# Layer 1, end of the first feed-forward: eight passes over one sequence's rows, on VectorE instead of GpSimd

## The chip, the cores and the metric

The kernel runs on one core of a Trainium2 chip. The metric is the device time of one execution in microseconds (us). TensorE (PE in the profile) multiplies, VectorE (DVE), ScalarE (ACT) and GpSimd (POOL) work element by element, and SyncE (SP) starts transfers. Each engine takes its own instructions strictly in order; between engines they wait for one another through semaphores.

## The reference, cut to what matters

The reference is a model of four "macaron" layers, all in float32, on 4 sequences of 512 positions with 128 features (2048 rows). In each layer a feed-forward block is applied at half weight, then an attention, then the same feed-forward block again. Layer 1 is

```python
x = x + 0.5 * ffn(layernorm(x))     # the first feed-forward
x = x + attn(layernorm(x))          # linear attention
x = x + 0.5 * ffn(layernorm(x))     # the same again

def ffn(x):                          # L1_ffn
    x1  = layer_norm(x + masked_softmax_attention(x), ln1_w, ln1_b)
    g   = softmax(x1 @ gate_w.T + gate_b)               # 8 experts, the best 2 are kept
    moe = sum over the best 2 of g_e * (x1 @ expert_w[e] + expert_b[e])
    return layer_norm(x1 + moe, ln2_w, ln2_b)

def attn(x):                         # L1_attn, 16 heads of 8
    q, k, v = l2norm(x @ Wq), l2norm(x @ Wk), x @ Wv
    scores  = (q @ k.T) * sigmoid(x @ Wb + bb) * lower_triangle
    return (scores @ v) @ Wo
```

So each sequence passes through two normalizations with a weight and a bias (`ln1`, `ln2`) and one residual sum in each feed-forward block. These are the steps that the change touches.

## The kernel before, in words

The whole model is one program. `x` (the residual stream) and `y` (a work copy of the same shape) lie in on-chip memory as 128 partitions by 16 tiles by 128 features; one sequence `b` (0 to 3) is four of those tiles (`TB` = 4), that is 128 x 512 elements. `yb` and `xb` are the slices of one sequence.

The first feed-forward of layer 1 (`l1_ffn`, called "l1f") runs the masked attention sequence by sequence, heads in groups. When a sequence is done, `finish` adds the attention's result to `y` and calls `l1_experts(b)`. That function doesn't do its work at once. It puts a list of small steps on a *chain* of this sequence (`spare(gap, step)`), and the main loop's `tick()` runs the next step of each chain when its gap has passed. In this way the experts of one sequence are spread through the attention of the next ones. The last two sequences, 2 and 3, don't end in time for that: their chains are handed on to the next stage, the linear attention `l1_attn`, and go on between its steps. In that stage everything that VectorE and ScalarE are given stays in the order in which the program issues it (`ordered["dve"]`, `ordered["act"]`), and TensorE's products as well. GpSimd's instructions are placed by their dependences.

Names and lines of the profile that are needed below:

- `affine(n)`: `scaled_by_act` lets ScalarE subtract the mean and divide by the deviation, four tiles in place (L316), and then two passes over 128 x 512 elements multiply by the weight (L1149) and add the bias (L1150) on `eng`. `eng` is GpSimd for sequences 0 to 2.
- `residual()`: `x += y` for the sequence, L1229, on `eng`.
- For sequence 3 in the linear attention `normed_in_parts(n, gap)` does the same in smaller steps: statistics in two halves, the scaling on ScalarE in two pairs of tiles (L1246), then the weight (L1253) and the bias (L1254) on GpSimd. It is called for `ln1` and for `ln2`. The residual sum of sequence 3 is L1270.
- `leave_normed(b, ...)`: after the residual sum the statistics of `x` (the plain layer norm ahead of the next block), on VectorE, the root of the variance (L234 on POOL or on DVE, and the power on POOL, L235), the scaling to `y` on VectorE, and `turn(b)`, TensorE's transposes into `pt_y` with ScalarE's copy (L326).
- In `l1_attn`: `project` (`pq_1a` on PE, `sq` and `km` on ACT, L1326 and L1327), `roots` and `unit_norm` on DVE (`rn`, `ir`, `km`), `to_features` (`pt_1a` on PE, `qkT` and `qm` on ACT, L1380 and L1383), `scores` (`ps_1a` on PE; half of `PT` by DVE, half by ACT, L1400, and then a mask on POOL, L1401), `with_values` (`po_1a`, `pst` on PE; `state` on DVE and on POOL, L1428) and `output` (`pz_1a` on PE, the sum into `x` on DVE).

All of VectorE's instructions are recorded under L186 and TensorE's under L202 (products) and L199 (transposes), because helpers issue them.

Of the kernel before, what the change touches and what calls it, by code (L numbers as in the profile page):

```python
# [29 lines left out]
B, S, D, H, HD = 4, 512, 128, 16, 8  # L30
NT = B * S // P
TB = S // P
# [25 lines left out]
class Columns:  # L58
# [50 lines left out]
VEC = Columns([  # L109
    ("1f_bv", 128), ("1f_bo", 128), ("ln1w", 128), ("ln1b", 128), ("ln2w", 128), ("ln2b", 128),  # L110
    ("gate_b", 8), ("1a_bb", 16), ("2f_rb", 8), ("3a_bv", 128), ("3a_bo", 128),
    ("3f_s0", 256), ("3f_s1", 256),
])
# [4 lines left out]
def tile_macaron(ctx, tc, x_in, const_in, vec_in, w0_in, ws_in, ws3_in, w2f_in, w3_in, out):  # L118
    nc = tc.nc
# [38 lines left out]
    vec = keep.tile([P, VEC.n], F32, name="vec")  # L158
# [34 lines left out]
    vector = InOrder()  # L193
# [27 lines left out]
    def rows(ap, n):  # L221

        return ap[:, None, :].to_broadcast([ap.shape[0], n, ap.shape[1]])
# [58 lines left out]
    ordered, routed = {"act": False, "dve": False, "results": False}, {}  # L282

    def by_order(i):
        if ordered["act"]:
            tc.keep_in_program_order(i)

    def statistics_in_parts(src, b):

        got = []  # L290

        def half(i):
            if not i:
                for tag, shape, bufs in (("ln_st", [P, TB, 6], 2), ("ln_mv", [P, TB, 2], 3), ("ln_r", [P, TB], 3)):
                    got.append(keep.tile(shape, F32, tag=tag, name=tag, bufs=bufs))
            st, mv, r = got
            for t in (2 * i, 2 * i + 1):
                vector.bn_stats(st[:, t, :], src[:, b * TB + t, :])
                vector.bn_aggr(mv[:, t, :], st[:, t, :])
            if i:  # L300
                inverse_root(keep, r, mv[:, :, 1], "ir4", ALU.add, 1e-5, nc.gpsimd)

        return got, (lambda: half(0), lambda: half(1))

    def scaled_by_act(dst, src, b, stats):

        mv, r = stats
        m = keep.tile([P, TB], F32, tag="ln_m", name="ln_m", bufs=3)
        if gathering(b):
            vector.scalar_tensor_tensor(m, mv[:, :, 0], -1.0, r, ALU.mult, ALU.mult)  # L310
        else:
            nc.gpsimd.tensor_mul(m, mv[:, :, 0], r)
            nc.gpsimd.tensor_scalar_mul(m, m, -1.0)
        for i in range(TB):
            t = b * TB + i
            by_order(nc.scalar.activation(dst[:, t, :], src[:, t, :], AF.Identity, scale=r[:, i : i + 1], bias=m[:, i : i + 1]))  # L316
# [4 lines left out]
    def turn(b):  # L321

        pt = bank("m", "pt_y")
        for t in range(TB):
            transpose_in_order(pt[:, ts(t, P)], y[:, b * TB + t, :])
        by_order(nc.scalar.copy(yT[:, b, :], pt))  # L326
# [6 lines left out]
    def chain(b):  # L333
        parts = deque()
        chains.append([b, clock[0], parts])
        return lambda gap, f, products=True: parts.append((gap, f, products))
# [14 lines left out]
    def leave_normed(b, spare, gap, pinned=False, start=1, to_route=True):  # L351

        st = []

        def scale():
            scaled(y, x, b, st[-1] if pinned != "parts" else st[0][1:], pinned is True)
            ready.add(b)

        if pinned == "parts":
            got, halves = statistics_in_parts(x, b)  # L360
            st.append(got)
            spare(start, halves[0], False)
            spare(1, halves[1], False)
            spare(2, scale, False)
        else:
            spare(start, lambda: st.append(statistics(x, b)), False)
            spare(1, scale, False)
        spare(gap, lambda: turn(b))
        if routed and to_route:
            spare(1, lambda: logits(b))  # L370
            if b % 2:
                first, second, third = route(b // 2)
                spare(1, first, False)
                spare(routed["gaps"][0], second)
                spare(routed["gaps"][1], third)
# [715 lines left out]
    def l1_ffn(tag, xb, l1_tiles, begun=None, besides=()):  # L1091

        with pool(tag) as sb, banks(tag + "ps", **MIX):
# [35 lines left out]
            def finish(b, pr):  # L1129
                yb = y[:, ts(b, TB), :]  # L1130
                vector.tensor_add(yb, yb, pr)
                l1_experts(xb, b)
# [3 lines left out]
    def l1_experts(sb, b):  # L1136


        yb, xb = y[:, ts(b, TB), :], x[:, ts(b, TB), :]
        ew, eb = WS(ws, "ew"), WS(ws, "eb")  # L1140
        st = {}
        eng = vector if b == B - 1 else nc.gpsimd

        def statistics_of_y():
            st["y"] = statistics(y, b, eng)

        def affine(n):
            scaled_by_act(y, y, b, st["y"])
            eng.tensor_mul(yb, yb, rows(VEC(vec, f"ln{n}w"), TB))  # L1149
            eng.tensor_add(yb, yb, rows(VEC(vec, f"ln{n}b"), TB))  # L1150

        def gates():
            pl = bank("m", "pl")
# [43 lines left out]
        def products(t):  # L1197
            pe = two_banks("pe1")
            for half in range(2):
                mm_in_order(pe[half], yT[:, b, ts(t, P)], ew[:, ts(half, 512)])  # L1200
            st["pe", t] = pe

        def sum_up(pe, t, n, a=0):
            yt = y[:, b * TB + t, :]
            for e in range(a, n):
                vector.scalar_tensor_tensor(yt, pe[e // 4][:, ts(e % 4, D)], st["g"][:, t, e : e + 1], yt, ALU.mult, ALU.add)
# [19 lines left out]
            experts(t)  # L1226

        def residual():
            eng.tensor_add(xb, xb, yb)  # L1229

        def normed_in_parts(n, gap):

            got, halves = statistics_in_parts(y, b)
            m = []

            def means():
                _, mv, r = got
                m.append(keep.tile([P, TB], F32, tag="ln_m", name="ln_m", bufs=3))
                nc.gpsimd.tensor_mul(m[0], mv[:, :, 0], r)
                nc.gpsimd.tensor_scalar_mul(m[0], m[0], -1.0)  # L1240

            def scale(i):
                r = got[2]
                for t in (2 * i, 2 * i + 1):
                    yt = y[:, b * TB + t, :]
                    by_order(nc.scalar.activation(yt, yt, AF.Identity, scale=r[:, t : t + 1], bias=m[0][:, t : t + 1]))  # L1246

            spare(gap, halves[0], False)
            spare(1, halves[1], False)
            spare(1, means, False)  # L1250
            spare(1, lambda: scale(0), False)
            spare(1, lambda: scale(1), False)
            spare(0, lambda: nc.gpsimd.tensor_mul(yb, yb, rows(VEC(vec, f"ln{n}w"), TB)), False)  # L1253
            spare(1, lambda: nc.gpsimd.tensor_add(yb, yb, rows(VEC(vec, f"ln{n}b"), TB)), False)  # L1254

        spare = chain(b)
        if b == B - 1 and not routed:
            normed_in_parts(1, 1)
            spare(3, lambda: turn(b))
            spare(2, gates)  # L1260
            for f, gap in ((share, 1), (best, 1), (two_best, 1)):
                spare(gap, f, False)
            spare(1, turn_gates)
            spare(2, biases)
            for t in range(TB):
                spare(1, lambda t=t: products(t))
                spare(0, lambda t=t: sum_up(st["pe", t], t, 4), False)
                spare(1, lambda t=t: sum_up(st.pop(("pe", t)), t, 8, 4), False)
            normed_in_parts(2, 1)
            spare(1, lambda: nc.gpsimd.tensor_add(xb, xb, yb), False)  # L1270
            leave_normed(b, spare, 2, "parts", 2)
            return
        spare(2, statistics_of_y, False)
        spare(4, lambda: affine(1), False)
        spare(4, lambda: turn(b))
        alone = b == B - 1 and routed
# [10 lines left out]
        for t in range(TB):  # L1287
# [4 lines left out]
            else:  # L1292
                spare(2, lambda t=t: both(t))
        spare(1, statistics_of_y, False)
        spare(4, lambda: affine(2), False)
        spare(2, residual, False)
        leave_normed(b, spare, 2)

# [964 lines left out]
    with pool("ws") as wp:  # L2263
# [9 lines left out]
        with pool("l2x") as l2x:  # L2273
# [20 lines left out]
            with ExitStack() as first_layer:  # L2294
                xb = first_layer.enter_context(pool("l1x"))
# [43 lines left out]
            with pool("l2g") as sb, banks("l2gps", a=2, g=2, t=2, m=2):  # L2339
# [8 lines left out]
                while slots:  # L2348
                    n = slots[0][0]
# [163 lines left out]
```

## Time and profile before

| | |
|---|---|
| time, median of 4 runs | 2607.97 us (2600.35 to 2610.62) |
| the profiled execution: its time | 2608.76 us |
| the profiled execution: its span | 2606.9 us, so 1.9 us lie around the span |
| the linear attention of layer 1 in it | about 687.8 to 819.8 us of the span |
| in 680 to 820 us: busy PE, DVE, ACT, POOL | 103.6, 91.3, 66.4, 48.5 of 140 us |
| the eight passes that the change speaks of | 1.26 to 1.28 us each on POOL: five from 693.98 to 700.50 us, three from 755.97 to 759.91 us |

The profile's start times are us from the span's start. "busy" is the time in which an engine executes instructions, a "releaser" is the instruction that ended a wait, and PEclk is the clock that TensorE was granted, 1.00 being full speed. The share of an engine over the span says little here, since the change concerns some 70 us of 2607.

### The profile page before, as it was taken

Reading aid. Unit: us, or ns where it says so; the run is one execution under the profiler, and the core shown is the slowest. Engines: PE = TensorE matmul, PEld = TensorE weight load, DVE = VectorE, ACT = ScalarE, POOL = GpSimd, SP = SyncE. Lnnn points to the kernel's source line nnn. Section 1 sums busy time; section 2 is a strip of 40 time slices with the busy share of each in tenths; the row PEclk is TensorE's granted clock in tenths of the full one; section 3 lists DMA queues with packets and bytes.
Section 4 is the critical chain, followed back from the end, with each engine's and each line's share of the span. In section 5 each row is a group of like instructions: output and inputs, shape, how many; then the busy total and the mean of one; then the engine's idle time right before and its main releaser. Section 6 shows DMA issues by size and latency. Waiting matters only on the chain.

```text
span 2606.9 us, 50965 instructions
## 1 busy us (share of the span) xinstructions
PE 2235.9 (86%) x19070; PEld 1274.1 (49%) x19070; DVE 1776.9 (68%) x4755; ACT 1335.4 (51%) x3271; POOL 945.9 (36%) x1519
## 2 busy tenths in 40 slices
PE   5578679988778999988768868999889999799998
PEld 2245334443344444468648836555533333456555
DVE  3755667777466777755655478887557775888874
ACT  4056205444443544434526338887615555588874
POOL 2022113233232222333332368676310000777761
PEclk9789789899689999889969879999889999899998
DMA  3052000000000000037325821110000000110100
GB/s 150 0 170 92 1 0 2 1 1 2 1 1 1 2 2 5 23 122 239 100 87 157 273 67 26 24 26 20 3 1 1 1 1 1 29 28 22 24 22 13
DMA packets 40142, 113.21 MB, mean 43 GB/s; under 512 B 7064, under 2 KB 16536, under 8 KB 39384
## 3 DMA queue, kind: packets, MB, share of 16 engines
q1 hardware_dynamic: 36520, 100.94, 12.2%
q0 software_dynamic: 2944, 6.04, 1.1%
q8 instruction: 151, 2.47, 0.4%
q10 hardware_dynamic: 432, 2.98, 0.3%
q14 instruction: 95, 0.78, 0.1%
HBM read 79.78 MB, written 15.47 MB: 37 GB/s over the span
## 4 chain that ended last, share of the span: by engine, by line
PE 59%; DVE 19%; POOL 11%; ACT 6%; issue 4%; DMA 1%; SPq 0%; POOLq 0%; DVEq 0%; ACTq 0%
PE pk_at L202 11%; PE po_at L202 6%; PE pa L202 4%; PE pq_at L202 4%; PE pag L202 3%; DVE t L186 3%; PE pz L202 3%; PE po L202 3%; PE pe L202 3%; PE idle L202 2%; PE pg L202 2%; DVE y L186 2%; POOL t L1985 2%; PE p_qk L202 2%; PE pt L199 2%
## 5 line engine op out<-in xcount | busy, mean ns | idle before, releaser
L942 ACT ACTIVATE PT<-pk_at 128x512 f32<-128x512 f32 (+3 forms) x768 | 335.2, 488 | 377.9 <-PE pq_at L202 239.0
L202 PE MATMUL pk_at<-qx,km 32*128 32x512 f32 (+3 forms) x1536 | 400.3, 558 | 5.6 <-ACT PT L942 3.0
L186 DVE CUSTOM_DVE_ANT_0 s<-pq_at,cst 128x384 f32<-128x384 f32 (+3 forms) x512 | 249.9, 488 | 98.7 <-PE pq_at L202 45.3
L202 PE MATMUL pq_at<-km,qT 32*128 32x128 f32 (+3 forms) x1024 | 274.6, 504 | 15.6 <-DVE nm L186 12.5
L1927 ACT ACTIVATE s<-s,nm,rn 128x128 f32<-128x128 f32 x512 | 245.6, 483 | 5.5 <-DVE nm L186 5.3
L945 POOL TENSOR_SCALAR_AFFINE_SELECT PT<-PT 128x256 f32<-128x256 f32 x256 | 104.6, 411 | 384.1 <-ACT PT L942 382.8
L202 PEld LDWEIGHTS pk_at<-qx,km 32*128 32x128 f32 x1536 | 146.8, 191 | 155.0 <-issue 90.8
L202 PE MATMUL po_at<-PT,vh 128*32 128x128 f32 (+3 forms) x2432 | 203.2, 393 | 3.4 <-POOL PT L945 3.3
L186 DVE TENSOR_REDUCE nm<-pq_at 128x1 f32<-128x512 f32 x256 | 164.9, 685 | 52.2 <-PE pq_at L202 50.8
L186 DVE TENSOR_TENSOR t<-p_qk,w 128x512 f32<-128x512 f32 (+1 forms) x192 | 155.2, 862 | 52.4 <-ACT sq L1927 50.1
L1985 POOL TENSOR_TENSOR t<-t,t 128x1024 f32<-128x1024 f32 x64 | 151.2, 2363 | 57.7 <-DVE t L186 46.8
L202 PE MATMUL pq_at<-km,t 32*128 32x512 f32 x512 | 163.9, 657 | 0.1
L202 PE MATMUL p_qk<-w,hT 128*128 128x512 f32 x256 | 133.5, 647 | 17.6 <-DVE hT L186 9.1
L2055 POOL TENSOR_TENSOR s<-s,sm 128x1024 f32<-128x1024 f32 x64 | 121.5, 1899 | 63.5 <-DVE sm L186 62.5
L235 POOL TENSOR_TENSOR ln_r<-ir,minus_half 128x4 f32<-128x4 f32 x60 | 61.9, 1033 | 207.1 <-DVE ir L186 203.9
L202 PEld LDWEIGHTS po_at<-PT,vh 128*32 128x32 f32 x2432 | 54.0, 110 | 169.3 <-issue 121.8
L202 PEld LDWEIGHTS pq_at<-km,qT 32*128 32x128 f32 x1024 | 110.5, 191 | 43.5 <-DVE nm L186 23.0
L326 ACT COPY yT<-pt_y 128x512 f32<-128x512 f32 x56 | 32.8, 585 | 181.8 <-PE pt_y L199 181.5
L199 PE MATMUL pt<-ident,s 128*128 128x128 f32 x640 | 91.6, 289 | 30.6 <-POOL s L2055 22.7
L1587 POOL DMA_INDIRECT xg<-yd,come x60 | 57.6, 960 | 158.1 <-PE pt_x L199 75.8
L186 DVE SCALAR_TENSOR_TENSOR y<-pe,g,y 128x128 f32<-128x128 f32 x240 | 80.9, 348 | 30.1 <-PE pe L202 23.8
L202 PE MATMUL pag<-h,w 128*128 128x512 f32 (+3 forms) x204 | 93.7, 604 | 4.8 <-DVE t L186 3.2
(444 smaller groups left out, 5265.4 us busy)
## 6 DMA issues: line engine op xcount, KB each, us to landing
wf<-in_w2f_dram SPq DMA_DIRECT2D x45, 836.0 KB, 4.7
vb<-v SPq DMA_DIRECT2D x112, 128.0 KB, 2.3
w<-in_w2f_dram SPq DMA_DIRECT2D x15, 836.0 KB, 7.7
skew<-qe SPq DMA_DIRECT2D x16, 512.0 KB, 3.5
rel<-skew SPq DMA_DIRECT2D x64, 128.0 KB, 3.4
od<-o SPq DMA_DIRECT2D x60, 64.0 KB, 6.7
w<-in_w_dram SPq DMA_DIRECT2D x1, 3200.0 KB
w<-in_w_dram SPq DMA_DIRECT2D x12, 173.0 KB, 6.0
```

Of the source, the lines that this page charges most:

```text
L186: i = op(*args, **kw)
L199: return nc.tensor.transpose(dst, src, ident[: src.shape[0], : src.shape[0]])
L202: tc.keep_in_program_order(nc.tensor.matmul(dst, lhsT=lhsT, rhs=rhs, start=start, stop=stop))
L235: pin(nc.gpsimd.tensor_tensor(dst, v, minus_half[:, :n], ALU.pow))
L326: by_order(nc.scalar.copy(yT[:, b, :], pt))
L942: by_order(nc.scalar.activation(PT[:, i, q0:], pk[:, q0:], AF.Exp, scale=SC8))
L945: nc.gpsimd.affine_select(d, d, pattern=[[0, 2], [1, P]], base=0, channel_multiplier=-1, compare_op=ALU.is_ge, fill=0.0)
L1587: nc.gpsimd.indirect_dma_start(xT[s], None, yds[k][:, :], bass.IndirectOffsetOnAxis(ap=come[:, i : i + 1], axis=0))
L1927: tc.keep_in_program_order(nc.scalar.activation(*args, **kw))
L1985: pool_in_order(nc.gpsimd.tensor_add(t1, t1, t2))
L2055: pool_in_order(nc.gpsimd.tensor_mul(s, s, bcast(s_state[step].pop("sm"), P)))
```

## The change

In the kernel before, for sequences 2 and 3 of the first feed-forward (the call where `routed` is empty), three kinds of pass over 128 x 512 elements ran on GpSimd. With the change they run on VectorE:

- sequence 2: the weight and the bias of `ln2` and the residual sum (3 passes)
- sequence 3: the weight and the bias of `ln1`, of `ln2`, and the residual sum (5 passes)

Sequences 0 and 1, `ln1` of sequence 2, and the second feed-forward of layer 1 stay as they were. Because VectorE keeps the program's order in the linear attention, the passes stand in its queue where the program issues them.

```diff
         eng = vector if b == B - 1 else nc.gpsimd
+        handed = b >= B - 2 and not routed
...
         def affine(n):
             scaled_by_act(y, y, b, st["y"])
-            eng.tensor_mul(yb, yb, rows(VEC(vec, f"ln{n}w"), TB))
-            eng.tensor_add(yb, yb, rows(VEC(vec, f"ln{n}b"), TB))
+            e = vector if handed and n == 2 else eng
+            e.tensor_mul(yb, yb, rows(VEC(vec, f"ln{n}w"), TB))
+            e.tensor_add(yb, yb, rows(VEC(vec, f"ln{n}b"), TB))
...
         def residual():
-            eng.tensor_add(xb, xb, yb)
+            (vector if handed else eng).tensor_add(xb, xb, yb)
...
             spare(1, lambda: scale(1), False)
-            spare(0, lambda: nc.gpsimd.tensor_mul(yb, yb, rows(VEC(vec, f"ln{n}w"), TB)), False)
-            spare(1, lambda: nc.gpsimd.tensor_add(yb, yb, rows(VEC(vec, f"ln{n}b"), TB)), False)
+            spare(0, lambda: vector.tensor_mul(yb, yb, rows(VEC(vec, f"ln{n}w"), TB)), False)
+            spare(1, lambda: vector.tensor_add(yb, yb, rows(VEC(vec, f"ln{n}b"), TB)), False)
...
             normed_in_parts(2, 1)
-            spare(1, lambda: nc.gpsimd.tensor_add(xb, xb, yb), False)
+            spare(1, lambda: vector.tensor_add(xb, xb, yb), False)
             leave_normed(b, spare, 2, "parts", 2)
```

## The prediction

> **What bounds the kernel now.** I read the page first, only to see how much the change can concern.
>
> ```profile
> PE 2235.9 (86%) x19070; PEld 1274.1 (49%) x19070; DVE 1776.9 (68%) x4755; ACT 1335.4 (51%) x3271; POOL 945.9 (36%) x1519
> PE 59%; DVE 19%; POOL 11%; ACT 6%; issue 4%; DMA 1%; SPq 0%; POOLq 0%; DVEq 0%; ACTq 0%
> ```
>
> TensorE carries most of the chain, GpSimd a ninth. Eight passes of about 1.3 us are 10 us of GpSimd in a span of 2607, so the question is local. I therefore asked for the chain of waits between 690 and 704 us, where five of the eight passes run.
>
> ```profile
> 692.25 1.66 ACT y L316 x4
> 693.98 1.28 POOL y L1149
> 695.33 1.27 POOL y L1150
> 696.67 1.26 POOL x L1229
> 697.93 1.23 POOL y L1253
> 699.23 1.27 POOL y L1254
> 700.55 1.12 PE pt_y L199 x4
> ```
>
> The columns are start, length, engine, tile and line. All five passes are on the chain, end to end: 6.5 us from ScalarE's scaling to the transposes of sequence 3. The timelines of TensorE and VectorE show who else waits (in brackets the idle time before the instruction and its releaser).
>
> ```profile
> 700.55 1.12 PE L199 MATMUL pt_y<-ident,y 128*128 128x128 f32 x4 [6.89 <-POOL y L1254]
> 702.92 1.15 PE L199 MATMUL pt_y<-ident,y 128*128 128x128 f32 x4
> ```
>
> ```profile
> 697.97 0.29 DVE L186 BATCH_NORM_STATS2 ln_st<-x 128x6 f32<-128x128 f32 x1 [6.79 <-POOL x L1229]
> ...
> 699.69 0.83 DVE L186 TENSOR_SCALAR ir<-ln_mv 128x4 f32<-128x4 f32 x1
> ...
> 701.67 1.87 DVE L186 TENSOR_SCALAR y<-x,ln_mv,ln_r 128x128 f32<-128x128 f32 x4
> ```
>
> Both engines stand idle nearly 7 us here. TensorE's second group of transposes, at 702.92, is that of sequence 2, whose `y` VectorE scales from 701.67 to 703.54. So two paths end together: sequence 3 through the bias at 700.50, and sequence 2 through the residual sum at 697.93, the statistics, the power on GpSimd and the scaling.
>
> The other three passes are at 755.97 to 759.91. There the chain doesn't go through them. It goes through VectorE's normalization of the keys:
>
> ```profile
> 754.00 1.22 DVE L186 TENSOR_TENSOR PT<-ps_1a,cst 128x1024 f32<-128x1024 f32 x1 [0.19 <-PE ps_1a L202]
> ...
> 758.63 0.69 DVE L186 TENSOR_REDUCE rn<-sq 128x64 f32<-128x512 f32 x1 [1.94 <-ACT sq L1326]
> 759.35 0.65 DVE L186 TENSOR_SCALAR ir<-rn 128x128 f32<-128x128 f32 x1
> ...
> 763.22 1.21 DVE L186 TENSOR_TENSOR km<-km,rn 128x1024 f32<-128x1024 f32 x1
> ```
>
> ```profile
> 764.58 0.66 PE L199 MATMUL pt_1a<-ident,km 128*128 128x128 f32 x2 [6.40 <-DVE km L186]
> ```
>
> TensorE waits 6.4 us for `km`. Whatever the change puts ahead of 758.63 in VectorE's queue can move that end.
>
> **Price of a pass on VectorE.** No pass of this kind runs on VectorE there, but a sum of two on-chip operands of the same size does, in the same stage:
>
> ```profile
> 798.71 0.69 DVE L186 TENSOR_TENSOR qin<-qin,t 128x512 f32<-128x512 f32 x1
> ```
>
> It takes 0.69 us, the next instruction starts 0.61 us after it, and where one needs the result of the last the start comes 0.04 us after its end (the 128x128 steps on `ir`: 0.29 long, 0.33 apart). So 0.61 to 0.73 us a pass against 1.34 on GpSimd.
>
> **First place, five passes.** In VectorE's queue they stand after `vm` (done at 691.2), and ahead of sequence 2's statistics, in the order weight 2, bias 2, weight 3, residual 2, bias 3. Nothing else is queued that was running in that time. Weight 2 starts at 693.97, when ScalarE has scaled sequence 2; bias 2 at 694.70, to 695.39. Weight 3 needs ScalarE's scaling of sequence 3, which runs 693.80 to 695.43, so 695.47. Residual 2 at 696.08, bias 3 at 696.69, to 697.38. TensorE's first transposes start at 697.4 instead of 700.55: 3.1 us earlier.
>
> The second path gains less. Sequence 2's statistics now stand behind bias 3 and start at 697.30, only 0.67 earlier. They take 1.72 us (697.97 to 699.69), so `ir` could start at 699.02. There it may meet GpSimd: before, `ir` (128x4) took 0.83 us and ended as L1254 ended, where 128x128 steps of that kind take 0.23 at 722 us. After the change the mask L1401 is free to run from 698.3, when ScalarE's `PT` is done (697.25 plus 1.02), to 699.4, and holds `ir` until then. The power (1.04 us) ends at 700.55, and the scaling starts at 700.6 instead of 701.67. Its four pieces took 1.87 us with a mask beside them (POOL L1401 at 701.60) and take 1.08 at 765.97 without one. The mask being over, I take 1.08: it ends at 701.7 instead of 703.54. The second transposes then end near 702.0 instead of 704.07. That is a gain of 2.0 us, with the bounds 1.1 (the scaling is held as before) and 3.1 (this path is no limit at all). From there to 750 us every queue keeps its order and each step waits for this one, so the 2.0 stays.
>
> **Second place, three passes.** They stand in VectorE's queue after the sum into `x` at 752.73: weight 3 and bias 3, then half of sequence 0's statistics, `PT`, the residual sum, the other half, `state`, `x`, and `rn`. Weight 3 must wait for ScalarE's last pair of L1246 (755.00 plus 0.88), so VectorE stands still from 753.0 to 755.9 where it worked before. Then: weight 755.94, bias 756.67, statistics 757.28, `PT` 758.1 (before: 754.0), residual 759.25, statistics 759.86, `state` and `x` 760.7, `rn` 761.13 instead of 758.63. That is 2.5 us late. But part comes back. Beside L1270 and the mask at 761.46 to 762.55 the steps from `ir` to `rn` took 3.74 us (759.35 to 763.09); the same steps took 2.36 at 721.92 to 724.28. With GpSimd's three passes gone, its mask runs at 758.1 and no longer beside them. So 2.5 less 1.4, and `km` is 1.1 late; with some of `state` on GpSimd (0.49 us at L1428) beside, 1.2. TensorE's wait grows from 6.4 to 7.6. Who else waits for the late `PT`? The product that reads it is at 767.9, behind `km` anyway; the banks that `state` and `x` free are wanted after 764. These cost nothing while `km` is later than them; without that cover `PT` would cost its whole 4.1. Bounds: 0 and 2.6.
>
> GpSimd's own queue loses 10.1 us of work and gains no wait; power and masks only move earlier. No transfer is issued in either place.
>
> [...] The row first: `ir` at 699.69, 0.83 us beside GpSimd and 0.23 elsewhere. [...] The rows place the masks at 698.3 to 699.4 and 758.1 to 759.2, ahead of or between the passes, so I add nothing for it.
>
> **The sum.** 2.0 less 1.2 is 0.8 us faster. On the profiled execution that is 2608.76 - 0.8 = 2608.0; this execution lies 0.8 above the median of the runs, and the median goes from 2607.97 to 2607.2. The runs before spread over 10 us, so 0.3% (7.8 us) is about what a measurement of this kernel can tell from no change. The bounds of the two places give -3.1 to +1.5.
>
> What no row bounds well is the granted clock. In the windows it is 0.5 or 1.0, and changes at 704.7, 711.5, 718.3, 725.2, 735.4, 759.3, 769.5: steps that are multiples of 3.4 us, up after such a stretch full of products, down after one that is mostly idle. A group of eight `ps_1a` takes 2.09 us at half and 1.14 at full clock. A stretch more or less at half clock is some 1.7 us. I allow two either way.
>
> **The rivals.**
> *The wait decides (slower).* VectorE's stop at 753.0 to 755.9 is on the path whole: none of the 1.4 us comes back (2.6 late), or `PT`, 4.1 late, holds TensorE; at the first place only 1.1 is won. That is 1.5 to 3.0 slower, and with two stretches at half clock up to 6.4: about 2611. It decides if `rn` after the change starts more than 2 us after ScalarE's `sq` and TensorE waits there over 8.5 us. For it speaks that VectorE must keep its order; against it that TensorE already waits 6.4 there.
> *The idle time closes (faster).* TensorE and VectorE lose their whole 3.1 us and `km` isn't late: 3.1, with one or two clock stretches 4.8 to 6.5, about 2603. For it: both engines idle at the first place; against it the power and the statistics that stay in the path.
> *The passes don't move.* Excluded: the order of the built program shows all eight in VectorE's queue.
>
> **The chances.** The forecast, within some 2 us of 2607.2, has 0.45. The slower rival has 0.27, of which 0.10 for over 0.3%, should late work and clock add up beyond my two stretches. The faster one has 0.28, of which 0.10 for over 0.3%. So 0.10, 0.80, 0.10. The range, from the faster case less the scatter of medians (2.5 us) to the slower one plus it, is 2600.5 to 2613.
>
> **What would show it.** Right: L1149 to L1254 gone from GpSimd in 694 to 700 us, five passes of 0.69 us on VectorE, TensorE's first wait near 3.7 instead of 6.89 us, the second transposes ending near 702; later VectorE idle for 2.9 us ahead of a weight pass that ScalarE's `y` L1246 releases, and TensorE's wait for `km` near 7.6. Wrong: passes of over 1 us (held by GpSimd), or a difference that builds up after 820 us, where no instruction moved.

## The result, and the profile after

The changed kernel takes 2611.46 us (median of 47 runs, 2605.79 to 2619.82), the kernel before on the same chip 2607.18 us (71 runs). The ratio is 1.0018, with a 95% interval of 1.0013 to 1.0023: 3.4 to 6.0 us slower, 4.7 in the middle (the medians themselves differ by 4.3). That is inside the 0.3% that I had called no change, and inside the range, but on the other side of zero from the forecast of 0.8 us faster. The profiled execution took 2614.8 us with a span of 2613.1. One run of the kernel before, on the chip of the last pair of experiments, took 3494.59 us at a granted clock of 0.55 and is left out of the ratios.

The page's busy times in the changed kernel:

```profile
PE 2235.5 (86%) x19070; PEld 1273.0 (49%) x19070; DVE 1779.5 (68%) x4763; ACT 1335.5 (51%) x3271; POOL 935.7 (36%) x1511
```

GpSimd lost eight instructions and 10.2 us, VectorE gained eight and only 2.6 us: the passes are shorter there, and some of its other steps became shorter too, as the rows below show. Nothing on the page tells why the kernel became slower. I looked at the two places, and they look almost exactly as forecast. TensorE's timeline at the first place:

```profile
697.85 1.09 PE L199 MATMUL pt_y<-ident,y 128*128 128x128 f32 x4 [3.85 <-ACT qm L1385]
...
701.45 1.15 PE L199 MATMUL pt_y<-ident,y 128*128 128x128 f32 x4 [1.17 <-DVE y L186]
```

It waits 3.85 us instead of 6.89, and the second transposes start at 701.45 instead of 702.92 (they now stand alone, after a wait of 1.17 us). VectorE's timeline there, columns as before:

```profile
694.27 2.23 DVE L186 TENSOR_TENSOR y<-y,vec 128x512 f32<-128x512 f32 x3 [2.75 <-ACT y L316]
696.42 0.68 DVE L186 TENSOR_TENSOR x<-x,y 128x512 f32<-128x512 f32 x1
697.02 0.69 DVE L186 TENSOR_TENSOR y<-y,vec 128x512 f32<-128x512 f32 x1
...
699.41 0.38 DVE L186 TENSOR_SCALAR ir<-ln_mv 128x4 f32<-128x4 f32 x1
...
700.96 1.11 DVE L186 TENSOR_SCALAR y<-x,ln_mv,ln_r 128x128 f32<-128x128 f32 x4
```

Five passes of 0.68 to 0.69 us (the first row merges three of them), started 0.60 to 0.82 us apart, where the forecast's own start times lie 0.61 to 0.77 apart; `ir` 0.38 instead of 0.83; the scaling 1.11 us instead of 1.87. At the second place VectorE and TensorE show:

```profile
758.14 1.42 DVE L186 TENSOR_TENSOR y<-y,vec 128x512 f32<-128x512 f32 x2 [2.90 <-ACT y L1248]
...
761.41 0.68 DVE L186 TENSOR_TENSOR x<-x,y 128x512 f32<-128x512 f32 x1
```

```profile
767.97 0.66 PE L199 MATMUL pt_1a<-ident,km 128*128 128x128 f32 x2 [7.58 <-DVE km L186]
```

VectorE stands still for 2.90 us, and TensorE waits 7.58 us for `km` instead of 6.40. Each of these was forecast. So the loss lies elsewhere.

**Where it comes from.** I took the start of the same ScalarE instruction in two profiles and subtracted. All differences are set to zero at 664 us, ahead of both places, because the start of the work differs between executions. At 701 us the changed kernel is 3.05 us early; at 757, before any instruction of the second place has acted on ScalarE's work, it is 1.91 late; at 832 it is 3.50 late, at 1050 2.48, and at 1130 6.11. From 1050 to 1130 us no instruction of the change lies.

The first of these turns is visible in the products that follow the transposes, ahead in the kernel before, then in the changed one:

```profile
705.39 1.14 PE L202 MATMUL ps_1a<-qm,qkT 32*128 32x512 f32 x8
706.46 1.08 PE L202 MATMUL po_1a<-PT,vm 128*32 128x128 f32 x32
```

```profile
704.46 2.09 PE L202 MATMUL ps_1a<-qm,qkT 32*128 32x512 f32 x8
706.48 1.94 PE L202 MATMUL po_1a<-PT,vm 128*32 128x128 f32 x32
```

The same products start 0.93 us earlier and take nearly twice as long. The table by windows says why; its columns are the window, its length, then busy time (and instructions) of PE, PEld, DVE, ACT and POOL, then the granted clock PEclk. Before, and after:

```profile
704.00:708.00 4.00, 4.00 (x54) 3.02 (x53) 2.10 (x7) 3.86 (x9) 0.00 (x0) 0.91 0.00 0
```

```profile
704.00:708.00 4.00, 4.00 (x43) 2.34 (x43) 1.95 (x6) 3.06 (x6) 0.27 (x1) 0.50 0.00 0
```

TensorE is busy throughout in both, at clock 0.91 before and 0.50 after. The clock went up at 704.7 before and at 708.5 after. In the profiles before and after, all changes of the clock (112 and 116) lie whole multiples of 3.41 us from one another: a fixed grid. The changes given below for e2, m0 and m1 do so too. In the changed kernel a step of the grid lies at 705.1; TensorE had been busy since 701.45, with transposes and 128 x 8 products, and the trace shows it busy for all 3.41 us ahead of that step, but the clock rose only one step later. Before, wider products (128 x 400) had filled part of the stretch ahead of 704.7. Being earlier moved the work to another place on the grid, and there the clock was worse. By 757 us the changed kernel has lost more than this: TensorE waits at about 741 us (it is busy for 1.45 of the 3.41 us ahead of 742.6), and its clock is halved from 742.6 to 749.5 us, where the kernel before has full clock from 735.5 to 759.3.

### The profile page after: what moved, and what is told of

Same layout as the page of the kernel before. It is cut to its first block, busy times and chain, and to the rows that moved or that the text cites. A ratio compares the mean times of both kernels' runs of the same rounds, so it can differ in the third digit from the quotient of the medians.

```text
span 2613.1 us, 50963 instructions
## 1 busy us (share of the span) xinstructions
PE 2235.5 (86%) x19070; PEld 1273.0 (49%) x19070; DVE 1779.5 (68%) x4763; ACT 1335.5 (51%) x3271; POOL 935.7 (36%) x1511
## 3 DMA queue, kind: packets, MB, share of 16 engines
q0 software_dynamic: 2944, 6.04, 1.1%
## 4 chain that ended last, share of the span: by engine, by line
PE 58%; DVE 19%; POOL 11%; ACT 5%; issue 5%; DMA 2%; SPq 0%; POOLq 0%; DVEq 0%; ACTq 0%
PE pk_at L202 11%; PE po_at L202 6%; PE pa L202 4%; PE pq_at L202 4%; DVE t L186 3%; PE pag L202 3%; PE pz L202 3%; PE po L202 3%; PE pe L202 2%; PE idle L202 2%; DVE y L186 2%; POOL t L1987 2%; PE pg L202 2%; PE pt L199 2%; DVE s L186 2%
```

## The experiments

There were 18 runs. Ratios are to the kernel before on the same chip. Two of the chips are some 5 to 8 us slower than the others (the kernel before takes 2615.65 us on the one where the d and h kernels ran, 2613.67 on that of the k kernels, 2607.2 to 2608.7 elsewhere), so times are compared within a batch only. The ratios come from all the runs of a batch and differ from the quotient of the medians by up to 0.09% (p6: 1.0008 by medians). The table gives, for each profile, how late the same ScalarE instruction is against the first profile of before (us, zero at 664 us). It ends at 1200 us because the profiles from the two slower chips lose 7 to 12 us more between 1200 and 1500 us. A profile is one execution: that of the changed kernel took 3.3 us more than its median, that of e4 was the fastest of its twelve runs.

| kernel | 757 | 832 | 1050 | 1110 | 1200 | ratio to before (95%) |
|---|---|---|---|---|---|---|
| before, again (e3) | -0.03 | -0.05 | -0.07 | -0.26 | -0.07 | 0.9989 (0.9979 to 0.9999) |
| after | +1.91 | +3.50 | +2.48 | +5.89 | +6.48 | 1.0018 (1.0013 to 1.0023) |
| after, again (e4) | -1.32 | +0.17 | -0.88 | +2.54 | +3.13 | 1.0008 (1.0000 to 1.0017) |
| first place alone (e1) | +1.89 | +2.85 | +3.62 | +5.44 | +6.04 | 1.0011 (1.0001 to 1.0020) |
| second place alone (e2) | -0.02 | +0.58 | +0.32 | +5.90 | +6.46 | 1.0021 (1.0010 to 1.0032) |
| one late pass (d1) | +0.02 | +0.17 | +0.33 | +5.93 | +6.48 | 1.0023 (1.0013 to 1.0034) |
| three late passes (d3) | -0.07 | +2.57 | +3.49 | +9.04 | +9.72 | 1.0020 (1.0009 to 1.0031) |
| before, held (h0) | +1.33 | +0.80 | +2.59 | +5.89 | +6.41 | 1.0024 (1.0013 to 1.0034) |
| after, held (h1) | +0.40 | +1.01 | +0.37 | +5.97 | +6.48 | 1.0024 (1.0014 to 1.0034) |
| before, small pause (p6) | -0.01 | +0.74 | +2.60 | +5.94 | +6.47 | 1.0017 (1.0006 to 1.0028) |
| before, middle pause (p16) | -0.09 | +1.83 | +0.24 | +5.84 | +6.37 | 1.0016 (1.0007 to 1.0025) |
| before, long pause (p34) | -0.07 | +3.48 | +3.39 | +5.11 | +3.82 | 1.0010 (1.0001 to 1.0019) |
| after, small pause (a3) | +1.77 | +3.83 | +3.33 | +4.76 | +3.73 | 1.0018 (1.0009 to 1.0026) |
| before, filled (k0) | +0.06 | +0.07 | +0.05 | +6.09 | +6.57 | 1.0031 (1.0018 to 1.0043) |
| after, filled (k1) | -1.36 | +0.14 | +0.32 | +3.22 | +3.42 | 1.0019 (1.0009 to 1.0029) |
| before, filled more (k2) | +0.03 | +0.03 | +0.01 | +3.18 | +3.40 | 1.0037 (1.0024 to 1.0050) |
| after, filled more (k3) | +1.93 | +3.53 | +2.51 | +9.07 | +9.83 | 1.0036 (1.0023 to 1.0049) |
| before, chain moved (m0) | +0.02 | +0.02 | +0.01 | -4.73 | -3.61 | 1.0012 (0.9994 to 1.0029) |
| after, chain moved (m1) | -1.38 | +0.10 | -0.93 | +7.35 | +7.34 | 1.0034 (1.0019 to 1.0048) |

**One place alone, and each kernel again.** First only the five passes of the first place (sequence 2's three, and `ln1` of sequence 3), then only the three of the second:

```diff
+ (vector if n == 1 else nc.gpsimd).tensor_mul(yb, yb, ...)   # e1; e2 has n == 2, with the kernel before elsewhere
+ (vector if n == 1 else nc.gpsimd).tensor_add(yb, yb, ...)
...
- vector.tensor_add(xb, xb, yb)                               # sequence 3, e1
+ nc.gpsimd.tensor_add(xb, xb, yb)
```

> Only the five passes of the first place (sequence 2: weight, bias and residual sum; sequence 3: weight and bias of the first normalization) run on VectorE; the three of the second place stay on GpSimd. Theory C (clock): the passes win about 2 us there, as forecast, but TensorE's clock changes on a grid of 3.4 us, so work that comes 2 us earlier meets other half-clock stretches, and these take the gain back: the median is 0 to 4 us slower than before (ratio 1.000 to 1.0015), and in the profile the stretches at half clock between 690 and 820 us are longer by some 3 us in sum. Theory W (the stop of VectorE at the second place costs everything): this one has no stop, so it is 1 to 2 us faster than before (ratio 0.9992 to 0.9997).

> Only the three passes of the second place (sequence 3: weight and bias of the second normalization, residual sum) run on VectorE. Theory C: TensorE waits 7.6 us for the normalized keys instead of 6.4, and the median is 1 to 2 us slower (ratio 1.0004 to 1.0008), with the clock as in the kernel before up to 758 us. Theory W: this place holds the whole loss, 4 to 6 us (ratio 1.0015 to 1.0023), by a wait longer than 8.5 us or by waits after it.

> The kernel before, once more, as a second profile and as a measure of what two equal kernels differ by. Theory C, if the clock's grid is tied to the program: the clock changes at the same places as in the first profile (704.7, 711.5, 718.3, 725.2, 735.4, 759.3, 769.5 us, within 0.4 us). If the grid runs free: other places, and another time between 690 and 820 us. Theory W says nothing on the clock. Ratio 0.9995 to 1.0005 by both.

> The kernel after, once more. Theory C with a grid tied to the program: again a half-clock stretch at 742.6 to 749.5 us, 2 us late at 757 us and 3.5 us late at 820 us against the kernel before. Theory C with a free grid: another pattern, the loss between 690 and 820 us anywhere from 0 to 5 us. Theory W: the wait for the keys is 7.6 us and the loss up to 757 us is not there in this profile. Ratio 1.0013 to 1.0023 by all.

Either place alone is slower (1.0011, 1.0021), and the two don't add up to more than one of them. The repeat of the kernel before gave 0.9989, so 0.1% (2.6 us) is nearer to what such a comparison can tell than its interval says. Of the first place, whose waits shrank by 3 us, these runs therefore show only that it does not win them. The second place alone cost as much as had been expected of a wait over 8.5 us or waits behind it (1.0015 to 1.0023), and more than had been expected of the clock (1.0004 to 1.0008). But TensorE waits 7.57 us for `km` there, the kernel is 0.58 us late at 832 us, and 5.6 of its 6.46 us come between 1050 and 1110 us, where no instruction of the change lies. The repeat of the changed kernel is the most telling profile: the same instructions as in "after", yet 757 us is reached 1.32 us early instead of 1.91 late.

**Late work alone, and TensorE held busy.** d1 and d3 put passes of 128 x 384 into an unread tile ahead of sequence 2's `km`, in VectorE's queue; h0 and h1 put three idle products of 128 x 512 into TensorE's wait at 741 us.

```diff
+ if b == 2:                                    # d1: one width, d3: three
+     late = sb.tile([P, 3, P], F32, tag="ir128", name="late", bufs=2).rearrange("p a b -> p (a b)")
+     for i, w in enumerate((384,)):
+         vector.tensor_add(late[:, :w], late[:, :w] if i else CT[:, :w], ST[:, :w])
...
+ for _ in range(3 if half and n == 4 else 0):  # h0, h1
+     idle_product("o", S)
```

> The kernel before with one pass of 128x384 more on VectorE, into a tile that nobody reads, right ahead of the product that normalizes sequence 2's keys (763 us). Nothing moves between engines; TensorE's wait for the keys grows by about 0.5 us. Theory C (the work's place on the clock's 3.4 us grid sets the loss): a shift as small as that of the second place alone costs as much, 3 to 6 us (ratio 1.0012 to 1.0023), most of it between 1048 and 1110 us, where no instruction differs. [...]

> The same with three such passes, about 1.7 us, half of a grid step. Theory C: not three times the loss of the one pass; anything from 0 to 8 us by how the work falls on the grid, with other half-clock stretches from 1000 us on. [...]

> The kernel before with the same three idle products, as the control. Theory C: no half-clock stretch was there, so nothing changes up to 820 us beyond 0.5 us (the products may end up to 0.3 us after the wait), and the median stays within 1 us, unless that small shift meets the grid as in the delayed kernels (then up to 5 us slower). [...]

> The kernel after with three idle products of 128x512 on TensorE in its wait at about 741 us (ahead of the second half of the scores of the linear attention's fifth step), so that the clock sees work there. Theory C: the half-clock stretch of 742.6 to 749.5 us goes, and at 757 us the kernel is 1.5 to 2 us ahead of the kernel before instead of 1.9 behind; with the second place's 1.2 it is 0.5 to 1 ahead at 820 us; the median over the whole kernel then depends on the grid after that, 1 us faster to 4 slower. [...]

One late pass delays 832 us by 0.17 us and costs 1.0023; three delay it by 2.57 us and cost 1.0020. That a pass costs its own length (some 0.5 us for the one and 1.7 for the three, by the expectations) is refuted. With TensorE held, the changed kernel is 0.93 us ahead of its control at 757 us (+0.40 against +1.33): with the clock up in both (PEclk 1.00 from 740 to 750 us), the first place does win. But the control itself lost 1.33 us there, where at most 0.5 was expected. Both end alike, and the control is as slow as the changed kernel.

**Pauses at one point.** Idle products at 823.5 us, at the start of the second masked attention: 256 wide, 512 and 256, three of 512, and 48 wide in the changed kernel.

```diff
-            for _ in range(3):
-                idle_product("o", S)
+            for n in (S, S, S, 512, 512, 512)[: 3 if besides else None]:   # p34; p6: 256; p16: 512, 256; a3: 48
+                idle_product("o", n)
```

> The kernel before with one idle product of 128x256 more on TensorE at 823.5 us, in the row of three that opens the second masked attention: a pause of about 0.5 us, after the linear attention, where the clock is up. Theory C (the place of the work on the clock's 3.4 us grid sets the loss): about as dear as the pass of 0.5 us at 763 us was, 3 to 6 us (ratio 1.0011 to 1.0024), nearly all of it between 930 and 1130 us. Theory D (each edit costs what its own instructions cost): 0.5 us, ratio 0.9998 to 1.0006.

> The same with a product of 128x512 and one of 128x256 more, a pause of about 1.6 us, half a grid step. Theory C: 2 to 7 us (ratio 1.0008 to 1.0027), and not three times the loss of the pause of 0.5 us. Theory D: 1.6 us, ratio 1.0003 to 1.0009.

> The same with three products of 128x512 more, a pause of 3.3 to 3.5 us, one grid step. Theory C: the longest pause costs no more than the shortest. If it meets the step within 0.1 us, the half-clock stretches after 830 us are those of the kernel before, one step later, nothing is lost between 1055 and 1130 us, and the whole is 3.4 us slower (ratio 1.0010 to 1.0016); if it misses, up to 6 more. Theory D: 3.4 us, ratio 1.0010 to 1.0016, and in the order of the pauses 0.5, 1.7, 3.4.

> The kernel after with one narrow idle product (128x48) more at the same place, a pause of 0.2 to 0.4 us. In its profile the kernel after was 3.1 us late against the clock's grid at 848 us, 0.3 short of a whole step. Theory C: the pause fills the step, nothing is lost between 1055 and 1130 us (3.6 us in the kernel after), and the kernel is 0 to 3 us faster than the kernel after although it does more (ratio to before 1.0008 to 1.0016); if the pause misses the step by over 0.1 us there is no gain. Theory D: 0.3 us slower than the kernel after (1.0014 to 1.0023).

A pause that moves 832 us by 0.74 us leaves the kernel 6.47 us late at 1200; one that moves it by 3.48 us, one step of the grid, leaves it 3.82 late. The changed kernel with a pause more is 2.75 us earlier at 1200 than without. So late work doesn't carry through as such: at 1200 us 18 of the 19 profiles of the table lie within 0.55 us of a whole number of steps (0, 3.41, 6.83 or 10.24 us late, or 3.41 early). The ratios (1.0010 to 1.0018) can't be told apart, so this rests on the profiles; a3's ratio is no lower than the changed kernel's, though up to 3 us had been expected.

**What makes 1050 to 1110 us so sensitive.** Between these two points the two profiles of before lose nothing, and 17 of the 18 others 1.4 to 8.3 us (m0 gains). The chain of waits in the kernel before shows work of the second feed-forward that runs beside the attention:

```profile
1067.16 1.26 ACT y L316 x3
...
1068.50 1.27 POOL y L1149
...
1069.84 1.27 POOL y L1150
...
1071.18 1.26 POOL x L1229
1072.44 1.23 POOL y L1149
1073.67 0.36 POOL PT L945
1074.03 1.24 POOL y L1150
```

GpSimd bounds this stretch: from 1069.5 to 1072.8 us it is busy for 3.14 of the 3.30 us, TensorE for 2.63, as the first window below shows. Compare the clock before and in e2, whose work is 0.32 us late at 1050 us. Before:

```profile
1069.50:1072.80 3.30, 2.63 (x20) 1.22 (x20) 0.32 (x2) 1.21 (x6) 3.14 (x4) 0.57 0.00 0
...
1083.00:1087.00 4.00, 4.00 (x38) 1.68 (x36) 2.62 (x10) 2.15 (x6) 0.81 (x2) 0.92 0.00 0
```

In e2:

```profile
1069.50:1072.80 3.30, 1.92 (x20) 0.77 (x20) 0.47 (x3) 1.85 (x7) 3.14 (x4) 1.00 0.00 0
...
1083.00:1087.00 4.00, 4.00 (x24) 1.15 (x20) 1.53 (x5) 1.26 (x3) 0.41 (x1) 0.56 0.00 0
```

The kernel before is halved at 1070.0, inside the stretch that GpSimd bounds, and is back at full clock at 1083.6. There the slow TensorE cost nothing: from the product that ends a wait of TensorE at the start of this stretch to its first product behind GpSimd's step it is 3.91 us in before (1070.17 to 1074.08) and 3.92 in e2 (1070.02 to 1073.94). In e2 the clock is still full until 1072.9, TensorE does its few products sooner and waits longer for the same GpSimd step, and is then slow until 1086.5, when it is what everything waits for. TensorE's timelines, before and e2:

```profile
1074.08 0.64 PE L202 MATMUL po_at<-PT,vh 128*32 128x128 f32 x4 [0.51 <-POOL PT L945]
...
1083.15 1.26 PE L202 MATMUL po_at<-PT,vh 128*32 128x512 f32 x8
```

```profile
1073.94 0.64 PE L202 MATMUL po_at<-PT,vh 128*32 128x128 f32 x4 [2.00 <-POOL PT L945]
...
1083.01 1.94 PE L202 MATMUL po_at<-PT,vh 128*32 128x512 f32 x8
```

The full clock at 1070 us bought 1.5 us more of waiting; the half clock at 1083 cost 0.68 us on this group alone. In e2, p16, h1 and d1 a second halving near 1095 to 1107 us follows, which the kernel before doesn't have (PEclk from 1090 to 1110 us: 1.00 before, 0.74 in e2, where TensorE is busy all 20 us), and by 1110 us they are 5.6 us later. Both kernels wait 1.33 us for `PT` just ahead of this. In before 1.1 us of that wait lie in the grid's stretch that ends at 1070.0, in e2 0.8 us in the one that ends at 1069.5 (worked out from the start of the next product and the changes of the clock). The same holds for all eleven profiles in which the clock stays full up to this wait and no product was added here: in before, e3, m0, a3 and p34 the stretch has 1.05 to 1.15 us without a product, and the clock is halved at its end; in e1, e2, d1, d3, h1 and p16 it has 0.70 to 0.92 us, and the clock is halved one step later. That small difference parts the two courses here, but it does not decide all: a3 and p34 are halved early too, get the full clock back after five steps instead of four, and lose 1.4 and 1.7 us by 1110.

**Filling that stretch.** Twelve idle products in it, in both kernels, 128 wide (k0, k1) or 256 wide (k2, k3):

```diff
                 elif masked and routed and n_steps - LEAD <= n < n_steps:
                     idle_product("q", S // 2)
+                elif masked and routed and n_steps - LEAD - 6 <= n < n_steps:
+                    idle_product("q", 128)    # k2, k3: 256
```

> The kernel before with an idle product of 128x128 in each half step of the six steps from about 1062 us on, near the end of the second masked attention (12 more products, some 0.2 us each at full clock, 2 us in all if none lies in a wait). If each edit costs its own instructions, 1 to 2 us slower than before. If the clock on its grid decides (C), the half clock from 1070.0 to 1083.6 moves or shrinks, and the time is that of before or up to 3.4 us more; the favourable place that the kernel before holds can be lost by this edit as by the others, about 2.5 to 6 us.

> The changed kernel with the same idle products. If the waits of this stretch make the loss between 1050 and 1130 us, it ends within 1 us of the kernel before with the same products; if VectorE's passes cost their own time, it stays about 4.7 us behind that kernel; if the sensitivity lies elsewhere, any distance between -3.4 and +6.8 us in whole steps of the clock's grid can be left.

> The kernel before with idle products of 128x256 in the same twelve places (some 0.3 us each at full clock, at most 4 us in all). By C the half clock of 1070.0 to 1083.6 us is shorter or gone, which is worth up to 5 us of the work there, and the products take 2 to 4 us: between 2 us faster and 4 us slower than before. If each edit costs its own instructions, 2 to 4 us slower.

> The changed kernel with the same larger idle products. By C it ends within 1 us of the kernel before with them, if they hold the clock in both; by the theory that the passes cost their own time, 4 to 5 us later than it.

The filling doesn't take the loss away: at 1200 us the four profiles are 3.4, 3.4, 6.6 and 9.8 us late, one, two and three steps of the grid. The medians rise by 4.6 to 11 us. That is more than either theory had allowed for k0 and k2. So the wait at 1068.8 us alone does not make the loss. But the pairs answer another question: edited alike, the changed kernel is not 4.7 us (0.18%) behind. It is 0.12% ahead in one pair (1.0019 against 1.0031; the intervals overlap, but the width of both together excludes 0.18% behind) and equal in ratio in the other (1.0036 against 1.0037, but five runs each, and by medians 2.5 us behind), as it was with TensorE held (1.0024 in both). This speaks against passes that cost their own time on VectorE: when the kernel before is edited too, it seems to lose its favourable place as well.

**Shortening the GpSimd chain.** The weight, bias and residual of the second normalization of sequences 1 and 2 in the second feed-forward go to VectorE, in both kernels:

```diff
+        late = routed and b >= 1                                # m0; m1: handed = b >= (1 if routed else B - 2)
...
+            e = vector if late and n == 2 else eng
+            e.tensor_mul(yb, yb, rows(VEC(vec, f"ln{n}w"), TB))
+            e.tensor_add(yb, yb, rows(VEC(vec, f"ln{n}b"), TB))
...
+            (vector if late else eng).tensor_add(xb, xb, yb)
```

> The kernel before with the weight, bias (second normalization) and residual sum of sequences 1 and 2 of the second feed-forward on VectorE, which waits 3.13 us for that residual at 1072.48 and 4.16 us at 1148.92. Three passes of 0.6 to 0.7 us for three of 1.34: 2 us off the chain at each place, up to 4 us in all if both stay. By the clock on its grid (C): at 1200 us between 4 us earlier and 6 us later than the kernel before, near a whole step of 3.4 us; the median between -4 and +5 us. If each pass moved is worth its own length: 4 us faster than before.

> The changed kernel with the same second change. By C: its distance to the kernel before with it is 0 or one or two steps of 3.4 us of either sign, since the stretch that the kernel before passes favourably is altered in both. If the passes of the first feed-forward cost their own time on VectorE, it stays about 4.7 us later than that kernel.

In its profile m0 is 4.73 us early at 1110 us. The clock in the windows of m0:

```profile
1070.00:1080.00 10.00, 8.95 (x56) 3.49 (x56) 8.90 (x30) 5.62 (x15) 5.67 (x7) 0.66 0.07 27
```

It is halved at 1070.8 and back at 1077.7 us, after two steps of the grid instead of four: TensorE has work without a gap from 1074.3 to 1077.7 us, where it waits 1.47 us in the same step of the kernel before. So the GpSimd chain is indeed what holds this stretch. In this profile the gain lasts (6.62 us early at 2590). But the other executions don't all have it: the profiled one took 2602.91 us, the median is 2610.91, m0's twelve runs go from 2597.46 to 2619.17 us, where all but one of the 23 of before on that chip lie between 2603.2 and 2611.8, and the ratio is 1.0012 (0.9994 to 1.0029). The changed kernel with the same edit is at full clock at 1080.8 too, but is halved again at 1094.4 and stays so to 1128.5 us; its median is 7.4 us above m0's. By medians alone this pair would fit passes that cost their own time. By the profile it does not: m1 is 0.10 us late at 832 us and falls behind only in that long halving, after 1090 us, where none of those passes lies. The two did not come together as I had expected of the grid theory, whose bounds were too wide here to be tested. Over the four pairs that were edited alike, h, the two of k and m, the changed kernel's ratio is 0.00, -0.12, -0.01 and +0.22% from its partner's (plus is slower); for the unedited pair, e3 and e4, it is +0.19%. No edited version was faster than the kernel before by its ratio.

## Why the prediction failed, step by step

- **Price of a pass, first wait, second path: right.** 0.68 to 0.69 us long, and 0.60 apart where nothing is waited for (forecast 0.61 to 0.73), a first wait of 3.85 us (3.7), second transposes ending at 702.6 (702.0), `ir` 0.38 us instead of 0.83, no mask beside the scaling (1.11, forecast 1.08). Nothing was added for passes beside GpSimd, and rightly: all eight took 0.68 to 0.69 us, and none lay beside an instruction of GpSimd for more than 0.05 us.
- **Second place: right.** VectorE still for 2.90 us (2.9), `km` 1.14 us late in e2, which has this place alone (763.89 against 763.22, plus the 0.47 that e2's work started earlier; forecast 1.2), TensorE's wait 7.58 us (7.6).
- **"From there to 750 us every queue keeps its order and each step waits for this one, so the 2.0 stays": wrong.** The order was kept, but the time wasn't. Seven profiles have the first place on VectorE and no idle product ahead of 757 us. In three of them (e4, k1, m1) 1.32 to 1.38 us are left at 757 us; in the other four (after, e1, a3, k3) the same instructions are 1.77 to 1.93 us late. They part where the clock comes back: in k1 at 731.1 us, in after at 735.8, which is one step of the grid and the 1.3 us that k1's work started earlier. The window that follows in after, then in k1:

```profile
732.00:736.00 4.00, 4.00 (x38) 2.40 (x36) 1.40 (x4) 0.00 (x0) 0.46 (x1) 0.52 0.00 0
```

```profile
732.00:736.00 4.00, 4.00 (x44) 2.46 (x43) 3.15 (x10) 1.03 (x3) 0.46 (x1) 1.00 0.00 0
```

  In the stretch of the grid before that, TensorE is busy throughout in all seven. Its group of products `ps_1a` starts 0.88 us ahead of the stretch both in k1, which gets the full clock at the stretch's end, and in k3, which doesn't. So here not even the place on the grid tells what the clock will do. In the favourable course the two places together give +0.10 to +0.17 us at 832 us, against a forecast of -0.8; in the other +3.5. So the sum was off by one microsecond in the one course of the clock and by four in the other.
- **The clock, "I allow two either way": wrong in kind and in size.** I treated it as noise that falls to both sides. But the kernel before isn't drawn at random: it passes 1050 to 1110 us in both its profiles without the loss that nearly all others show (the filled kernels' own products lie there too), and e2, d1, h1 and p16, within 0.4 us of it at 1050, lose 5.6. So any edit was more likely to lose than to win there. From 664 to 1200 us the changed kernel lost 6.48 us against a sum of -0.8: more than two stretches of 1.7. The sign of error that I had named, a difference that builds up after 820 us, came in part: 3.50 of the 6.48 us were there at 832 us.
- **The slower rival gave about the right time (2611) for the wrong reason.** It put the loss at VectorE's stop ahead of 756 us and needed TensorE to wait over 8.5 us there. TensorE waits 7.58, and the first place alone, without that stop, is slower too. The faster rival would have needed both engines' whole 3.1 us; the second transposes start 1.47 us earlier (1.79 with the zero at 664 us). By its own terms the slower rival reached to 2614.4 (6.4 above 2608.0), so the range, which ended at 2613, was a little short on that side.

What stays open: why the same instructions take one course at 732 us in three profiles and the other in four (their place on the grid at 664 us doesn't part them either: 13.01 to 13.07 us ahead of a clock change in the three, 12.87 to 13.07 in the four); which later stretches, beyond 1200 us, make up each median (e4 is 3.13 us late at 1200 in its profile and 0.88 at 2590, the changed kernel 6.48 and 5.02); and by what m1 falls into the long halving that m0 escapes. The course of the clock is shown for single executions; for the medians it is the theory that fits these runs best, not one that they prove.

## What to carry to other kernels

When TensorE's clock changes on a grid, here of 3.41 us, a gain or loss of one or two microseconds ahead of it is not a number to add: ask in which stretch of the grid the idle time will lie afterwards, and run a control that shifts the work without doing anything. Where the version at hand holds a good course by a narrow margin (here 0.32 us of lateness at 1050 us went with 5.6 us more by 1110), such shifts are to be priced on the losing side. And a half clock cost nothing here where GpSimd set the pace (the same step took 3.91 us at half clock in before and 3.92 in e2, where the clock was full for most of it); what mattered was when the full clock was back (1083.6 against 1086.5 us).

## What the hardware showed that I had not expected

- **Work and grid keep step.** At 664 us the same ScalarE instruction lies 12.87 to 13.09 us ahead of the same clock change in all 20 profiles, although its own start, counted from the span's, goes from 659.3 to 665.3 us. So up to there the executions differ by 6.0 us, but the place of the work on the grid of 3.41 us repeats within 0.22 us, and in e2 a shift of a tenth of a grid step at 1050 us (0.32 us) went with a loss of 5.6 us by 1110.
- **The length of a wait does not tell whether the clock is halved.** The kernel before is halved at 1070.0 us after a stretch of the grid with 1.1 us of waiting in it, the rest filled with narrow products. By the trace it is halved at 1110.9 us after a stretch without any waiting (busy for 3.41 of 3.41 us), and keeps full clock at 786.7 after one with 1.62 us (busy for 1.79). What else decides, no run here shows.
- **A pass on VectorE took 1.56 us beside one on GpSimd.** In m0 VectorE's residual sum meets a GpSimd pass. This is one such meeting; no other was looked at. VectorE's timeline, then GpSimd's:

```profile
1070.54 0.68 DVE L186 TENSOR_TENSOR y<-y,vec 128x512 f32<-128x512 f32 x1
...
1071.34 1.56 DVE L186 TENSOR_TENSOR x<-x,y 128x512 f32<-128x512 f32 x1
```

```profile
1070.91 1.44 POOL L1151 TENSOR_TENSOR y<-y,vec 128x512 f32<-128x512 f32 x1 [2.67 <-ACT y L316]
```

  The sum takes 1.56 us instead of 0.68, and ends 0.55 us after GpSimd's pass, as if it had started only with that pass's end at 1072.35. GpSimd's pass, which began beside VectorE's of 1070.54, took 1.44 instead of 1.27 us. In the changed kernel no moved pass lay beside one for more than 0.05 us, and they stayed at 0.68 to 0.69.
